# A bidirectional image scan on one core: one product for two taps of the causal convolution, and columns from blocks of 32

## The chip, the cores and the metric

The kernel runs on one core of a Trainium2 chip. The metric is the device time of one execution in microseconds. A profiled execution gives one trace; its span runs from the first instruction of the program to the last.

## The reference, cut to what matters

Layer 0 scans every image of `x` (8 images, 64 channels, 128 x 128) along its rows and along its columns, each in both directions:

```python
def mamba(seq, p):                       # seq: sequences x 128 tokens x 64
    xz = einsum('blc,ec->ble', seq, in_w)
    x, z = xz[..., :di], xz[..., di:]    # di = 128
    x = silu(causal_conv(x, conv_w, conv_b))      # 4 taps along the sequence, per channel
    xdbl = einsum('bld,ed->ble', x, xp_w)
    dt, Bm, Cm = split(xdbl)                       # 4, 16, 16 wide
    delta = softplus(einsum('blr,dr->bld', dt, dt_w) + dt_b)
    # per token: h = exp(delta*A)*h + (delta*x)*B ;  y = <h, C> + x*D    (16 states a channel)
    y = selective_scan(x, delta, -exp(A_log), Bm, Cm, Dp) * silu(z)
    return einsum('bld,cd->blc', y, out_w)
def run_bidir(seq, p):
    return 0.5 * (mamba(seq) + flip(mamba(flip(seq))))
x_rec = 0.5 * (rows(run_bidir) + columns(run_bidir))
x = silu(group_norm(x_rec)) + x
```

Layer 1 is a residual block of two 3 x 3 convolutions with batch norm on the result. All is float32. The input projection `in_w` and the four taps of `causal_conv` are both linear in the tokens, so their composition is four products, each with the tokens shifted by 0 to 3.

## The kernel before, in words

Work is cut into chunks of four sequences (`SEQ`), 512 tokens (`N`). An image has 32 row chunks and then 32 column chunks (`NCH` = 32), so there are 512 chunks in all. A chunk has 16 steps: step r takes one pair of channel halves (`half`), one group of four states (`ng`) and one direction (`d`) by `where(r)`. The loop `for s in range(total + UN)` issues the steps in an order written out by hand, and every engine runs its own instructions in that order. In text below, a step's number in brackets says for which step a piece of work is done: `drive(10)` is the drive for step 10.

For each step there are:

- `decay`: ScalarE (ACT) writes the edge (L360) and two exponentials (L363) into `dA`, one of two PSUM buffers, one step ahead of the scan. It may start once the scan two steps before has read its `dA`.
- `drive`: VectorE (DVE) multiplies `du` by `pb`, B spread over the partitions (L372), one step ahead. For steps 2, 5, 9, 12 and 15 (`GPS`) GpSimd (POOL) does it, from `bt`, which a DMA brings.
- `scan`: DVE scans 1024 elements (L380 forward, L382 backward).
- `weigh`: POOL multiplies the states by C (L387).
- `b_rows`, in even steps for the two steps that follow: TensorE makes `pb` (L352), into the one PSUM buffer of the tag "b". It waits until the last reader of that buffer is done.
- `add_up`, in even steps, four steps behind: TensorE sums states into `yp` (L403).

Beside the steps of chunk n, `prepare` makes what chunk n+1 needs, one piece per step from step 0 to 13:

- step 0: for a column chunk, ACT copies the chunk's columns out of the image in SBUF, `xc` (L252);
- steps 1 to 4: the products `cp` (L234 for rows, L240 for columns, called in `project`), two taps of one direction in each step;
- step 5: `u` (SiLU of `cp`, L265) and SiLU of the chunk's `sz`; step 6: `dp` (L272); step 7: `bp` (L277, tag "b") and its copy `bc` by ACT (L282), which a DMA stores as `bd` (L284);
- step 8: softplus (L287); step 9: `du` by DVE (L299), `dl` by ACT (L301) and eight DMAs to `dd` (L294); steps 10 to 13: eight DMAs that bring `dl` and `du` back, each channel repeated four times (L323); step 13: `zp` (L240 or L234, tag "b") and its copy `sz` (L314).

`cp`, `dp`, and the outputs `op` and `cps` share one PSUM buffer of two banks (tag "pt"). In step 3 DVE gates the chunk before (`y`, L410), in step 4 TensorE begins the next `yp` with u times D (`dg`, L393), and at steps 10 to 12 the chunk before is projected out: `op` (L416; for columns L421 adds what the rows left), copies by ACT (L429, L434), and for columns statistics by DVE (`gst`, L438). Group norm and the first convolution (`conv1`, L493 to L507) of the image before run in steps 5 and 7, and 14 to 2, of row chunks.

The whole image lies in SBUF as `xt`, the lower half of its rows on partitions 64 to 127, so a product takes 128 partitions of which the weights of one half are zero; a column chunk takes two products per tap, one for each half of the rows. The next image is loaded in the last two chunks. Nearly all DMAs are issued on SyncE's (SP's) queue, in program order; `fetch` brings `c` and `bt` some steps ahead.

## Time and profile before

| | |
|---|---|
| runs, median (lowest to highest) | 27046.4 us (27022.64 to 27052.52), 3 runs |
| profiled execution, its own time | 27036.85 us |
| its span, mean granted TensorE clock | 27035.1 us, 0.878 |
| busy: DVE, POOL, PE, ACT | 25638.5, 25139.5, 19433.8, 18477.9 us |
| products `cp`: L234 (rows), x4096 | 2022.6 us, 617 ns each |
| products `cp`: L240 (columns), x8192 | 2068.0 us, 397 ns each |
| copy `xc`, L252, x256 | 159.4 us, 623 ns each |
| DMA queues, share of 16 engines | 51.9% on SP's, 180 GB/s over the span |

A row of the profile names line, engine, operation, output and inputs, and how often. The busy time is the union of a group's instructions; the mean is of one, and instructions overlap, so count times mean can exceed it. A product in float32 appears as two records. "Idle" is the time in which the engine did nothing just before an instruction, and the name behind the arrow is what ended it. The scans run from 126 to 25907 us; what follows is the tail of the last image and layer 1's second convolution.

### The profile page before, as it was taken

To read this page: it belongs to the slowest core of one execution; us is meant where nothing else is said; L and a number is where in the kernel's file an instruction comes from. 1 tells how busy PE (TensorE), PEld (TensorE's weight loads), DVE (VectorE), ACT (ScalarE), POOL (GpSimd) and SP (SyncE) were. 2 spreads that over 40 slices of the span, in tenths; PEclk is the share of its full clock that TensorE was granted. 3 is DMA by queue.
4 is the path that set the end of the run, shared out by engine and by line. 5 is a ranking of instruction groups with operands and counts; after the bars stand their busy time and mean duration, and the time that the engine had idled before them with its cause. 6 is when DMAs were issued, how large, how long until landed. Compare 5 with 4: busy or idle time off the path is not lost.

```text
span 27035.1 us, 235698 instructions
## 1 busy us (share of the span) xinstructions
PE 19433.8 (72%) x65580; PEld 6667.4 (25%) x65580; DVE 25638.5 (95%) x15633; ACT 18477.9 (68%) x31150; POOL 25139.5 (93%) x10916
## 2 busy tenths in 40 slices
PE   5777777777777777777777777777777777777776
PEld 1222222222222222222222222222222222222222
DVE  8999999999999999999999999999999999999942
ACT  5777777777777777777777777777777777777732
POOL 7999999999999999999999999999999999999930
PEclk8888888888988889888898888988898888988888
DMA  5555555555555555555555555555555555555545
GB/s 180 174 180 172 184 191 183 177 173 184 194 179 176 172 189 192 178 174 172 194 188 177 175 177 193 184 181 171 179 197 178 178 173 182 198 177 179 170 141 188
DMA packets 2165564, 4871.20 MB, mean 180 GB/s; under 512 B 265856, under 2 KB 413456, under 8 KB 2148368
## 3 DMA queue, kind: packets, MB, share of 16 engines
q1 hardware_dynamic: 2143648, 4754.51, 51.9%
q10 hardware_dynamic: 15984, 68.06, 0.9%
q0 software_dynamic: 4608, 33.56, 0.3%
q8 instruction: 517, 8.47, 0.1%
q14 instruction: 807, 6.61, 0.1%
HBM read 4115.52 MB, written 738.98 MB: 180 GB/s over the span
## 4 chain that ended last, share of the span: by engine, by line
DVE 35%; PE 22%; issue 18%; ACT 12%; DMA 9%; SPq 2%; POOL 1%; DVEq 0%; POOLq 0%; ACTq 0%
DVE s L372 15%; DVE s L382 9%; DVE s L380 8%; DMA du<-dd 7%; PE pb L352 6%; ACT dA L363 6%; PE yp L403 5%; PE cps L665 2%; PE dp L272 2%; DVE du L299 2%; PE op L421 1%; PE op L416 1%; DVE y L410 1%; PE bp L277 1%; ACT xp L434 1%
## 5 line engine op out<-in xcount | busy, mean ns | idle before, releaser
L387 POOL TENSOR_TENSOR s<-s,c 128x1024 f32<-128x1024 f32 x8192 | 19151.8, 2365 | 659.6 <-DVE s L382 290.8
L363 ACT ACTIVATE dA<-dl,A 128x508 f32<-128x508 f32 x16384 | 11274.9, 688 | 518.0 <-ACT dA L360 3.1
L352 PE MATMUL pb<-u,wb 128*128 128x512 f32 x8192 | 5455.4, 753 | 6516.4 <-DVE s L372 5728.6
L382 DVE TENSOR_TENSOR_SCAN s<-dA,s 128x1024 f32<-128x1024 f32 x4096 | 9284.9, 2276 | 45.2 <-ACT dA L363 42.1
L380 DVE TENSOR_TENSOR_SCAN s<-dA,s 128x1024 f32<-128x1024 f32 x4096 | 9281.8, 2276 | 0.0
L372 DVE TENSOR_TENSOR s<-du,pb 128x1024 f32<-128x1024 f32 x5632 | 6742.2, 1197 | 132.7 <-DMA du<-dd 88.4
L372 POOL TENSOR_TENSOR s<-du,bt 128x1024 f32<-128x1024 f32 x2560 | 6071.0, 2371 | 149.6 <-DMA bt<-bd 147.3
L403 PE MATMUL yp<-s,fold 128*32 128x512 f32 x32768 | 5196.3, 712 | 5.2 <-POOL s L387 5.2
L360 ACT COPY dA<-zeros 128x8 f32<-128x8 f32 x8192 | 1381.9, 169 | 5321.8 <-DVE s L382 3465.4
L352 PEld LDWEIGHTS pb<-u,wb 128*128 128x128 f32 x8192 | 1522.2, 219 | 9638.4 <-DVE s L372 3874.8
L234 PE MATMUL cp<-xt,wc 128*128 128x512 f32 (+3 forms) x4096 | 2022.6, 617 | 119.1 <-DMA xt<-x_h 76.7
L240 PE MATMUL cp<-xc,wc 128*128 128x256 f32 (+3 forms) x8192 | 2068.0, 397 | 0.0
L240 PEld LDWEIGHTS cp<-xc,wc 128*128 128x128 f32 x8192 | 1585.9, 199 | 1029.5 <-issue 459.6
L403 PEld LDWEIGHTS yp<-s,fold 128*32 128x32 f32 x32768 | 692.5, 116 | 3780.4 <-issue 1996.7
L363 ACT ACT_TABLE_LOAD x1030 | 1321.5, 1283 | 26.7 <-DMA dl<-dd 8.4
L234 PEld LDWEIGHTS cp<-xt,wc 128*128 128x128 f32 x4096 | 766.7, 198 | 1424.5 <-issue 1242.4
L272 PE MATMUL dp<-u,wd 128*128 128x512 f32 x2048 | 983.5, 603 | 1.2 <-ACT u L265 1.2
L393 PE MATMUL yp<-u,dg 128*128 128x512 f32 x2048 | 961.9, 592 | 1.7 <-DVE y L410 1.7
L694 POOL DMA_DIRECT2D out<-cc x32 | 17.2, 538 | 979.0 <-ACT cc L693 979.0
L434 ACT COPY xp<-op 64x256 f32<-64x256 f32 x512 | 317.5, 620 | 887.6 <-PE op L421 884.6
L416 PE MATMUL op<-y,wo 128*128 128x512 f32 x1024 | 821.8, 895 | 0.9 <-DVE y L410 0.9
L493 PE MATMUL cps<-strip,w 128*128 128x512 f32 x1536 | 770.9, 629 | 48.9 <-DMA strip<-x_d 41.1
(109 smaller groups left out, 10548.3 us busy)
## 6 DMA issues: line engine op xcount, KB each, us to landing
dl<-dd SPq DMA_DIRECT2D x2048, 512.0 KB
du<-dd SPq DMA_DIRECT2D x2048, 512.0 KB
c<-bd SPq DMA_DIRECT2D x4096, 256.0 KB
bt<-bd SPq DMA_DIRECT2D x2560, 256.0 KB
dd<-du SPq DMA_DIRECT2D x2048, 128.0 KB
dd<-dl SPq DMA_DIRECT2D x2048, 128.0 KB
bd<-bc SPq DMA_DIRECT2D x512, 128.0 KB
c_d<-cs SPq DMA_DIRECT2D x256, 256.0 KB
```

Of the source, the lines that this page charges most:

```text
L234: nc.tensor.matmul(ps[:, :, lo:hi], lhsT[hf], xt[:, r : r + SEQ, lo - s : hi - s], start=start, stop=stop)
L240: nc.tensor.matmul(ps[:, :, lo:hi], lhsT[hf], g["xc"][:, :, lo - s - hf * HH : hi - s - hf * HH], start=start and hf == 0, stop=stop and h ...
L272: nc.tensor.matmul(dp[:, d, :], w["wd"], u[:, d, :], start=True, stop=True)
L352: nc.tensor.matmul(pb, wt[g["o"]]["wb"][:, P * ng : P * (ng + 1)], g["u"][:, d, :], start=True, stop=True)
L360: nc.scalar.copy(dA[:, :, :, edge], zeros)
L363: nc.scalar.activation(dA[:, j, :, t], dl[:, j, :, t], AF.Exp, scale=wt[g["o"]]["A"][:, 2 * half + j, ng : ng + 1])
L372: engine.tensor_mul(s, g["du", half, d], b.unsqueeze(1).to_broadcast([P, 2, N]))
L380: nc.vector.tensor_tensor_scan(s, a, s, 0.0, ALU.mult, ALU.add)
L382: nc.vector.tensor_tensor_scan(s[:, ::-1], a[:, ::-1], s[:, ::-1], 0.0, ALU.mult, ALU.add)
L387: nc.gpsimd.tensor_mul(s, s, c.unsqueeze(1).to_broadcast([P, 2, N]))
L403: nc.tensor.matmul(g["yp"][32 * q : 32 * (q + 1), :], fold, s[:, j, :], start=False, stop=r == UN - 2, skip_group_check=True,)
L416: nc.tensor.matmul(op, w["wo"].rearrange("p h c -> p (h c)"), g["y"], start=True, stop=o == 0)
```

## The change

A chunk's tokens no longer come from an image in SBUF. `stack` writes them twice into `xs`, one of two buffers that chunks use in turn: on partitions 0 to 63 as they are and on partitions 64 to 127 a token later, with columns of zeros on both sides. A product over 128 partitions then makes two taps, with weights laid out to match (`shift`), and a direction takes two products, whether rows or columns. `zp` takes the lower 64 partitions alone.

For a row chunk the two copies are DMAs from DRAM. For a column chunk ACT copies the columns to `xc` (`columns`, now at the head of step 0 of the chunk two before, ahead of `decay`), and four DMAs carry them to the stack. They are issued in step 2 of the chunk two before. The columns come from blocks of 32 (`CB`), two of which lie in SBUF; `load_columns` brings a quarter of a block at step 4 of every second chunk, from image chunk 22 on. In `prepare` the first three pieces are empty, and the products stand in steps 3 and 4. `xt` and its loads are gone.

```diff
--- before
+++ after
@@ -19,6 +19,7 @@
 HH = W // 2
 N = 512
 SEQ = N // W
+CB = 32
 NCH = W // SEQ
 NS = 16
 NQ = 4
@@ -26,7 +27,13 @@
 NTAP = 4
 EPS = 1e-5
 LAG = 4
+PAD = 2
 GPS = (2, 5, 9, 12, 15)
+
+
+def shift(d, k, e):
+
+    return 2 * k + e if d == 0 else 2 * k + 1 - e
 
 
 @with_exitstack
@@ -75,15 +82,15 @@
             cw = prep.tile([P, NTAP, P], F32, name="cw")
             nc.scalar.dma_start(out=cw, in_=p["conv_wT"].partition_broadcast(P))
 
-            wc = const.tile([P, 2, NTAP, P], F32, name=f"wc{o}")
-            wz = const.tile([P, 2, P], F32, name=f"wz{o}")
-            nc.vector.memset(wc, 0.0)
-            nc.vector.memset(wz, 0.0)
-            for hf in range(2):
-                h = slice(hf * C, (hf + 1) * C)
-                for j in range(NTAP):
-                    nc.vector.tensor_mul(wc[h, hf, j, :], inw[h, 0:P], cw[h, j, :])
-                nc.vector.tensor_copy(wz[h, hf, :], inw[h, P : 2 * P])
+
+            wc = const.tile([P, 2, 2, P], F32, name=f"wc{o}")
+            for d in range(2):
+                for k in range(2):
+                    for e in range(2):
+                        h = slice(e * C, (e + 1) * C)
+                        nc.vector.tensor_mul(wc[h, d, k, :], inw[h, 0:P], cw[h, NTAP - 1 - shift(d, k, e), :])
+            wz = const.tile([C, P], F32, name=f"wz{o}")
+            nc.vector.tensor_copy(wz, inw[0:C, P : 2 * P])
 
             xpr = prep.tile([4, P], F32, name="xpr")
             nc.sync.dma_start(out=xpr, in_=p["xp_w"][0:4, :])
@@ -210,57 +217,67 @@
         psa = st.enter_context(tc.tile_pool(name="psa", bufs=1, space=PSUM))
         psm = st.enter_context(tc.tile_pool(name="psm", bufs=1, space=PSUM))
 
-        xt = big.tile([P, HH, W], F32, name="xt")
         xp = big.tile([P, HH, W], F32, name="xp")
         strips = []
         for k in range(2):
             strip = big.tile([P, SEQ + 1, W + 2], F32, name=f"strip{k}")
             nc.vector.memset(strip, 0.0)
             strips.append(strip)
+        stacks = []
+        for k in range(2):
+            xs = big.tile([P, SEQ, PAD + W + 3], F32, name=f"xs{k}")
+            nc.vector.memset(xs, 0.0)
+            stacks.append(xs)
         zeros = big.tile([P, 2, SEQ], F32, name="zeros")
         nc.vector.memset(zeros, 0.0)
 
-        def load_image(b, k):
-
-            rows = slice(k * (HH // 8), (k + 1) * (HH // 8))
-            nc.sync.dma_start(out=xt[:, rows, :], in_=x[b].rearrange("p (h w) -> p h w", w=W)[:, rows, :])
-
-        def project(ps, lhsT, g, s, start, stop):
-
-            ps = ps.rearrange("p (q t) -> p q t", t=W)
-            if g["o"] == 0:
-                hf, r = divmod(SEQ * g["i"], HH)
-                lo, hi = max(s, 0), W + min(s, 0)
-                nc.tensor.matmul(
-                    ps[:, :, lo:hi], lhsT[hf], xt[:, r : r + SEQ, lo - s : hi - s], start=start, stop=stop
-                )
-                return
-            for hf in range(2):
-                lo, hi = max(hf * HH + s, 0), min((hf + 1) * HH + s, W)
-                nc.tensor.matmul(
-                    ps[:, :, lo:hi], lhsT[hf], g["xc"][:, :, lo - s - hf * HH : hi - s - hf * HH],
-                    start=start and hf == 0, stop=stop and hf == 1, skip_group_check=True,
-                )
+        def load_columns(b, k, j):
+
+            if j == 0:
+                blocks[b, k] = big.tile([P, HH, CB], F32, name="xb", bufs=2)
+            rows = slice(j * (HH // 4), (j + 1) * (HH // 4))
+            nc.sync.dma_start(
+                out=blocks[b, k][:, rows, :],
+                in_=x[b].rearrange("p (h w) -> p h w", w=W)[:, rows, CB * k : CB * (k + 1)],
+            )
+
+        def columns(g):
+
+            if g["o"] == 1:
+                k, i = divmod(SEQ * g["i"], CB)
+                g["xc"] = work.tile([P, SEQ, HH], F32, name="xc", bufs=1)
+                nc.scalar.copy(g["xc"], blocks[g["b"], k].rearrange("p h w -> p w h")[:, i : i + SEQ, :])
+
+        def stack(g, k):
+
+            xs = g["xs"] = stacks[k % 2]
+            for e in range(2):
+                es = slice(e * C, (e + 1) * C)
+                if g["o"] == 0:
+                    hf, r = divmod(SEQ * g["i"], HH)
+                    src = x[g["b"]].rearrange("p (h w) -> p h w", w=W)[hf * C : (hf + 1) * C, r : r + SEQ, :]
+                    nc.sync.dma_start(out=xs[es, :, PAD + e : PAD + e + W], in_=src)
+                else:
+                    for hf in range(2):
+                        t = PAD + e + hf * HH
+                        nc.sync.dma_start(out=xs[es, :, t : t + HH], in_=g["xc"][hf * C : (hf + 1) * C])
 
         def prepare(g, before):
 
 
             w = wt[g["o"]]
-            if g["o"] == 1:
-                g["xc"] = work.tile([P, SEQ, HH], F32, name="xc", bufs=1)
-                i = SEQ * g["i"]
-                nc.scalar.copy(g["xc"], xt.rearrange("p h w -> p w h")[:, i : i + SEQ, :])
+            yield
+            yield
             yield
             cp = psm.tile([P, 2, N], F32, name="cp", tag="pt")
             for d in range(2):
-                for s in range(NTAP):
-                    j = NTAP - 1 - s
-                    project(
-                        cp[:, d, :], [w["wc"][:, 0, j, :], w["wc"][:, 1, j, :]], g,
-                        s if d == 0 else -s, s == 0, s == NTAP - 1,
+                for k in range(2):
+                    t = PAD - 2 * k if d == 0 else PAD + 2 * k + 1
+                    nc.tensor.matmul(
+                        cp[:, d, :].rearrange("p (q t) -> p q t", t=W), w["wc"][:, d, k, :],
+                        g["xs"][:, :, t : t + W], start=k == 0, stop=k == 1,
                     )
-                    if s % 2:
-                        yield
+                yield
             u = work.tile([P, 2, N], F32, name="u")
             nc.scalar.activation(u, cp, AF.Silu, bias=w["conv_b"])
             if before is not None:
@@ -309,7 +326,9 @@
             replicate(g, 0, 1)
             yield
             zp = psa.tile([P, N], F32, name="zp", tag="b")
-            project(zp, [w["wz"][:, 0, :], w["wz"][:, 1, :]], g, 0, True, True)
+            nc.tensor.matmul(
+                zp.rearrange("p (q t) -> p q t", t=W), w["wz"], g["xs"][0:C, :, PAD : PAD + W], start=True, stop=True
+            )
             g["sz"] = work.tile([P, N], F32, name="sz")
             nc.scalar.copy(g["sz"], zp)
             replicate(g, 1, 1)
@@ -517,7 +536,7 @@
         OUT = 10
         NORM = (5, 7)
         CONV = (14, 15, 0, 1, 2)
-        LOAD = (2, 4, 6, 8)
+        blocks = {}
         gs = [dict(b=b, o=o, i=i) for b in range(B) for o in range(2) for i in range(NCH)]
         total = UN * len(gs)
         stats = {}
@@ -540,8 +559,8 @@
             return 2 if r == GPS[0] else 3
 
         with tc.manual_schedule():
-            for k in range(8):
-                load_image(0, k)
+            stack(gs[0], 0)
+            stack(gs[1], 1)
             for _ in prepare(gs[0], None):
                 pass
             for s in range(-9, 0):
@@ -557,6 +576,8 @@
                     for _ in pieces:
                         pass
                     pieces = prepare(gs[n + 1], gs[n]) if n + 1 < len(gs) else iter(())
+                if r == 0 and n + 2 < len(gs):
+                    columns(gs[n + 2])
                 if s + 1 < total:
                     decay(*at(s + 1))
                     if (s + 1) % UN not in GPS:
@@ -586,8 +607,10 @@
                 fetch(s)
                 if r == CONV[-1] and n % PER == 6:
                     next(conv3, None)
-                if r in LOAD and live and n % PER >= PER - 2 and gs[n]["b"] + 1 < B:
-                    load_image(gs[n]["b"] + 1, LOAD.index(r) + 4 * (n % 2))
+                if r == 2 and n + 2 < len(gs):
+                    stack(gs[n + 2], n + 2)
+                if r == 4 and n % 2 == 0 and NCH - 10 <= n % PER < PER - 10:
+                    load_columns(n // PER, *divmod((n % PER - NCH + 10) // 2, 4))
                 if r == OUT and prev:
                     output = emit(prev)
                     next(output)
```

## The prediction

> **What bounds the kernel now.** I read the page's busy shares first, then who waits for whom, then the timeline of single chunks. Over the span:

> ```profile
> PE 19433.8 (72%) x65580; PEld 6667.4 (25%) x65580; DVE 25638.5 (95%) x15633; ACT 18477.9 (68%) x31150; POOL 25139.5 (93%) x10916
> PEclk8888888888988889888898888988898888988888
> ```

> Between the first scan (126 us) and the last (25907 us) DVE is busy for 25382 us of 25781: it is the bound, POOL (25097) is just behind it, and TensorE has slack. The starts of the scans give 49.07 us as the shortest chunk. So a change to TensorE's work counts only through DVE's waits, some 400 us in all:

> ```profile
> DVE gst L438 <- ACT xp L434: 225.0, 209, 4.1
> DVE s L372 <- DMA du<-dd: 88.4, 124, 11.4
> DVE s L382 <- ACT dA L363: 42.1, 112, 0.4
> DVE s L372 <- PE pb L352: 32.6, 94, 1.5
> ```

> (total us, times, longest.) The last row is what the change aims at: mostly `drive(4)` waiting for its `pb`, which TensorE starts late behind the `cp` products of steps 1 and 2.

> ```profile
> 2232.41 1.10 PE L352 MATMUL pb<-u,wb 128*128 128x512 f32 x2 [1.81 <-DVE s L372]
> 2233.34 1.88 PE L272 MATMUL dp<-u,wd 128*128 128x512 f32 x4
> 2236.03 1.03 PE L277 MATMUL bp<-u,xpT 128*32 128x512 f32 x4
> ...
> 17266.57 1.74 PE L352 MATMUL pb<-u,wb 128*128 128x512 f32 x2 [1.86 <-DVE s L372]
> 17268.10 2.97 PE L272 MATMUL dp<-u,wd 128*128 128x512 f32 x4
> 17271.89 1.03 PE L277 MATMUL bp<-u,xpT 128*32 128x512 f32 x4
> ```

> (start, us, what; in brackets the idle time before.) With 1.81 us of idleness before step 6 the products ran at full clock; with 1.86 us they ran slow, `bp` came 1.7 us later, and ACT and DVE show who paid:

> ```profile
> 17272.96 0.58 ACT L282 COPY bc<-bp 64x512 f32<-64x512 f32 x1 [2.06 <-PE bp L277]
> 17274.83 1.22 DVE L372 TENSOR_TENSOR s<-du,pb 128x1024 f32<-128x1024 f32 x1 [0.72 <-PE pb L352]
> ```

> The windows of busy time confirm the clock (the column before the last two):

> ```profile
> 2232.40:2237.10 4.70, 4.65 (x18) 1.42 (x18) 4.70 (x3) 4.22 (x8) 4.70 (x3) 1.00 0.00 0
> 17266.90:17270.30 3.40, 3.40 (x5) 1.35 (x4) 3.40 (x3) 3.29 (x6) 3.40 (x3) 0.50 0.00 0
> ```

> The path: `bp` holds the one buffer of tag "b" until ACT has copied it to `bc` (L282); only then `pb` for `drive(10)` may be written (L352), and DVE needs it. Besides the first chunk, 18 chunks in the trace had `bp` 1.24 to 1.70 us late, and DVE waited 0.25 to 0.72 us: a late `bp` costs its lateness less 0.98 us.

> [...]the trace's packets of 512, 256 and 4 bytes took 27, 15 and 9 ns[...].

> **The change, part by part.**

> *Products.* Before, `cp` is 16 records per chunk of 0.43 us (row, L234), or 32 of half the width (column, L240), 6.9 us at full clock, in four pieces at steps 1 to 4. After, it is 8 records, 3.4 us, in two pieces at steps 3 and 4. Direct gain: the waits for `pb` at step 2, by the trace 26.6 us of the 32.6. Indirect cost: the freed time becomes idleness just before step 6. Count t from the scan of step 0. At 5.6 TensorE gets to `pb(4)`; behind it stand `yp`, `cp`, `pb(6)`, `cp`, `dg`, `yp`: 1.0+1.0+1.8+1.0+1.8+1.8+1.0 = 9.4 us at full clock, so it ends at 15.0 and not at 16.6 as now. `pb(8)` can't start before `drive(7)` ends at 18.4. The idleness grows from 1.81 to 3.4 us, over the 1.9 that one window bears; `dp`, `yp` and `bp` then start at half clock.

> How often: at step 0 TensorE mostly comes out of a pause at half clock (0.53 in column chunks, 0.72 in row chunks). Its `pb` and `yp` then fill t = 0.2 to 4.3. A window fills to 0.86 if it begins between -0.24 and 1.36, 1.6 of 3.41 us: in 47% of chunks the clock is full by `pb(4)`. In the other 53% it rises only at t = 8.7 to 12, the half-speed time fills the pause, and step 6 runs at full clock as now; `pb(4)` at half clock takes 2.07 us, inside the scan's 2.28, so it costs nothing. In the 47%, the fifth window edge lies at 16.8 to 18.4, where the clock drops (not in some 5% of them). Edges after 17.95 (30%) leave a full window next: one slow window, `bp` 1.5 to 1.7 late, 0.6 us of stall as in the 18 chunks. The other 65% wait two windows, 5.2 to 6.3 us at half speed: 2.6 to 3.15 late, 1.9 us of stall. Mean: 0.47 x (0.30 x 0.6 + 0.65 x 1.9) = 0.67 us per chunk; for the 376 chunks without conv1's products 250 us. In the 128 chunks with them (image chunks 7 to 22) TensorE is more often at full clock by step 2 but also busier until then; bounds 0 and 0.95 us, I take 0.3: 38 us.

> *Copy xc* (L252, 623 ns x256) goes ahead of step 1's decay on ACT. ACT then idles 1.14 us until DVE's scan frees `dA`, so zero; uncovered, 160 us. Its one buffer was read 14 steps earlier.

> *DMAs.* Gone: 64 loads of `xt`, 512 KB. New, all on SP's queue: two of 128 KB per row chunk, four of 64 KB per column chunk, 128 block loads of 256 KB in 128-byte runs. SP spends some 0.5 us on an issue, 1 to 2.5 us per chunk; it waits 7389.5 us (511 times, 14.5 each) at L284 for `bc`, and the new issues stand before that point. Behind them stand `c` for steps 8 to 12, `bt` and `bd`; `c` waits for a buffer from POOL anyway. A column stack makes SP wait for ACT's copy of step 0, before the time at which `c(8)` gets its buffer; that the stack's own buffer be free takes `zp` of chunk n, done at step 13 of the chunk before. Each DMA also waits for the one eight places ahead of it in SP's order (eight semaphores in turn); between `bd` and `du<-dd` nothing is put in, so the critical stretch keeps its neighbours. Ring time over 16 engines: 512 x 27 ns = 0.9 us (row), 1024 x 15 = 1.0 us (column)[...]. They run around steps 1 to 4, eight steps before `dd` and the critical `du` (88.4 us of waits). Zero; bounds 0 and 500 us below.

> *Start and preparation.* The first `cp` waits for `xt` until 91.7 us and takes 10.07 us for 16 records; with 8 it ends about 5 us sooner, less 1 us for clearing the stacks (two memsets like `strip`'s 0.6 us): -4 us, bounds -6 and 0. DVE's fewer clears of weights lie beside the load of `p_w`: zero. The freed SBUF: zero.

> Sum: 250 + 38 - 27 - 4 = +257 us. The profiled execution took 27036.85 us, 9.6 below the median; 27294 by its own time, 27300 as a median.

> **The rivals.**
> *No change (17%).* TensorE isn't done early enough: it needs under 1.86 us of idleness before step 6. That is so if it enters step 2 at half clock in nearly every phase. Then -31 us, 27015. Against it: a clock of 0.97 to 0.99 in step 2.
> *Faster (13%).* The wait of `gst` (0 to 1.33 us) also hangs on where windows fall: five column chunks take 252.6 us, just 74 windows, so chunks lock to the grid. If the new pattern locks where the mean wait is 0.5 and not 0.88, 100 us go, and 31 as above: 26915. It decides where chunks of 49.55 us keep clear of the slow phases, and needs step 6's delay to be absent.
> *Slower by DMA (7%).* The new transfers push `du` by about 1 us in every chunk: 512 us, 27550. It decides only if they are still in the rings at step 10.
> If the stacks don't halve the products, PE's instructions would not fall; the instruction lists show `cp` at two per direction.

> **Numbers.** The likeliest case is 63%, 27300, its own range 27100 to 27480. With the rivals, 26990 to 27480. A measurement here tells about 0.2% (54 us) from no change: faster 0.16, same 0.18, slower 0.66.

> **What would show it.** The products' 4090.6 us (L234 and L240) fall to 512 x 3.44 = 1760, more where the clock is half, and PE's busy time to some 17100 to 17900; the waits for `pb` at step 2 vanish; ACT's wait for `bp` (176.8 us) rises over 500, DVE's wait for `pb` (32.6) to about 300, now at `drive(10)`; TensorE idles over 3 us before step 6 in half of the chunks, and the mean clock (0.878) falls. I'm wrong on the cause if `bp` is hardly ever late, or if DVE's longer wait is the one for `du`; wrong on the size if late `bp` is seen in far more or fewer than 47% of chunks, or mostly with one slow window.

## The result, and the profile after

The changed kernel takes 27359.22 us (median of 4 runs, 27340.04 to 27373.71), against 27042.92 us before (4 runs, 27022.64 to 27052.52). The ratio is 1.0118, with a 95% interval of 1.0105 to 1.0131: slower by 316 us, where 254 were forecast. The profiled execution has a span of 27371.9 us, 336.8 more than the one before.

The page of the changed kernel begins with the busy times, and shows the clock in forty slices:

```profile
PE 18899.4 (69%) x56876; PEld 5233.6 (19%) x56876; DVE 25699.2 (94%) x15629; ACT 18459.6 (67%) x31150; POOL 25149.2 (92%) x10916
PEclk8888888888888888888888888888888888888888
```

TensorE has 8704 records fewer but is busy for only 534 us less, since much of what is left runs slower: `pb`, `yp` and `dp` together are busy for 1224 us longer (L371, L422 and L289, before L352, L403 and L272). The mean clock fell from 0.878 to 0.830. DVE, the bound, is busy for 61 us more with no more work.

Who waits for whom on DVE, the rows that answer to those of before (total us, times, longest):

```profile
DVE s L391 <- PE pb L371: 279.3, 221, 2.1
DVE gst L457 <- ACT xp L453: 240.3, 254, 4.1
DVE s L391 <- DMA du<-dd: 79.1, 95, 11.6
DVE s L401 <- ACT dA L382: 36.2, 112, 0.4
```

One wait has grown much, that of `drive` for `pb`, from 32.6 to 279.3 us; the wait of `gst` for `xp` is 15 us longer, that of `drive` for `du` 9 us shorter. On ACT, the row for the copy that stands between `bp` and `pb` rose from 176.8 us to:

```profile
ACT bc L299 <- PE bp L294: 717.3, 478, 3.4
```

The timeline of TensorE in one row chunk, from `pb(4)` to `bp`, shows how that comes about. Steps 2 to 4 are one unbroken block at full clock (1.00 from 8118.52 to 8127.87 us); then comes a pause, in brackets, and then `pb(8)` and `dp` at half clock:

```profile
8118.52 1.12 PE L371 MATMUL pb<-u,wb 128*128 128x512 f32 x2 [1.49 <-DVE s L391]
8119.58 1.06 PE L422 MATMUL yp<-s,fold 128*32 128x512 f32 x8
8120.57 1.99 PE L276 MATMUL cp<-xs,wc 128*128 128x512 f32 x4
8122.41 1.02 PE L371 MATMUL pb<-u,wb 128*128 128x512 f32 x2
8123.26 1.89 PE L276 MATMUL cp<-xs,wc 128*128 128x512 f32 x4
8124.99 1.88 PE L412 MATMUL yp<-u,dg 128*128 128x512 f32 x4
8126.80 1.07 PE L422 MATMUL yp<-s,fold 128*32 128x512 f32 x8
8131.33 2.04 PE L371 MATMUL pb<-u,wb 128*128 128x512 f32 x2 [3.47 <-DVE s L391]
8133.17 3.62 PE L289 MATMUL dp<-u,wd 128*128 128x512 f32 x4
8136.72 1.40 PE L422 MATMUL yp<-s,fold 128*32 128x512 f32 x8
8137.95 1.02 PE L294 MATMUL bp<-u,xpT 128*32 128x512 f32 x4
```

`pb(8)` takes 2.04 us and `dp` 3.62 us, about twice as long as in the usual chunk of before (1.10 and 1.88). The windows of busy time give the clock, in the column before the last two, for the stretch from `pb(8)` to the start of `bp` and for the one after:

```profile
8131.40:8138.00 6.60, 6.60 (x16) 2.10 (x18) 6.57 (x4) 4.14 (x7) 6.60 (x4) 0.54 0.00 0
8138.20:8140.50 2.30, 1.62 (x6) 0.30 (x2) 0.81 (x1) 1.41 (x4) 2.30 (x2) 1.00 0.00 0
```

What ACT and DVE wait for in the same chunk:

```profile
8139.02 0.58 ACT L299 COPY bc<-bp 64x512 f32<-64x512 f32 x1 [3.36 <-PE bp L294]
8140.89 1.22 DVE L391 TENSOR_TENSOR s<-du,pb 128x1024 f32<-128x1024 f32 x1 [1.88 <-PE pb L371]
```

The stretch from the first scan to the last is 333 us longer (25780 to 26113), and two sums make this up. DVE's idle time there grew by 271 us (399 to 670). Its idle time in front of `drive(10)`, counted by step, rose from 8 to 292 us; that in front of `drive(4)`, which the prediction calls the wait at step 2, was 27 us and is gone. DVE's busy time there grew by 62 us (25381 to 25443); the last section says why.

### The profile page after: what moved, and what is told of

Its sections match the earlier page's. It is cut to its first block, busy times and chain, and to the rows that moved or that the text cites. A ratio compares the mean times of both kernels' runs of the same rounds, so it can differ in the third digit from the quotient of the medians.

```text
span 27371.9 us, 221652 instructions
## 1 busy us (share of the span) xinstructions
PE 18899.4 (69%) x56876; PEld 5233.6 (19%) x56876; DVE 25699.2 (94%) x15629; ACT 18459.6 (67%) x31150; POOL 25149.2 (92%) x10916
## 5 line engine op out<-in xcount | busy, mean ns | idle before, releaser
L382 ACT ACTIVATE dA<-dl,A 128x508 f32<-128x508 f32 x16384 | 11274.5, 688 | 518.6 <-DMA dl<-dd 2.0
L371 PE MATMUL pb<-u,wb 128*128 128x512 f32 x8192 | 5988.2, 821 | 7418.6 <-DVE s L391 6648.1
L391 DVE TENSOR_TENSOR s<-du,pb 128x1024 f32<-128x1024 f32 x5632 | 6748.9, 1198 | 384.9 <-PE pb L371 279.3
L422 PE MATMUL yp<-s,fold 128*32 128x512 f32 x32768 | 5519.5, 753 | 5.2 <-POOL s L406 5.2
L371 PEld LDWEIGHTS pb<-u,wb 128*128 128x128 f32 x8192 | 1581.2, 233 | 11407.7 <-DVE s L391 5262.2
L276 PE MATMUL cp<-xs,wc 128*128 128x512 f32 x4096 | 2097.8, 634 | 79.5 <-DMA xs<-x_h 79.5
L422 PEld LDWEIGHTS yp<-s,fold 128*32 128x32 f32 x32768 | 715.4, 120 | 4249.8 <-issue 2461.0
L289 PE MATMUL dp<-u,wd 128*128 128x512 f32 x2048 | 1351.5, 797 | 1.2 <-ACT u L282 1.2
L276 PEld LDWEIGHTS cp<-xs,wc 128*128 128x128 f32 x4096 | 784.7, 203 | 1515.7 <-issue 1423.9
L329 PE MATMUL zp<-xs,wz 64*128 64x512 f32 x1024 | 581.8, 647 | 583.5 <-DVE s L391 582.8
L453 ACT COPY xp<-op 64x256 f32<-64x256 f32 x512 | 317.4, 620 | 915.9 <-PE op L440 912.9
L299 ACT COPY bc<-bp 64x512 f32<-64x512 f32 x512 | 296.4, 579 | 717.3 <-PE bp L294 717.3
```

The source lines that it names most:

```text
L276: nc.tensor.matmul(cp[:, d, :].rearrange("p (q t) -> p q t", t=W), w["wc"][:, d, k, :], g["xs"][:, :, t : t + W], start=k == 0, stop=k == 1,)
L289: nc.tensor.matmul(dp[:, d, :], w["wd"], u[:, d, :], start=True, stop=True)
L371: nc.tensor.matmul(pb, wt[g["o"]]["wb"][:, P * ng : P * (ng + 1)], g["u"][:, d, :], start=True, stop=True)
L382: nc.scalar.activation(dA[:, j, :, t], dl[:, j, :, t], AF.Exp, scale=wt[g["o"]]["A"][:, 2 * half + j, ng : ng + 1])
L391: engine.tensor_mul(s, g["du", half, d], b.unsqueeze(1).to_broadcast([P, 2, N]))
L422: nc.tensor.matmul(g["yp"][32 * q : 32 * (q + 1), :], fold, s[:, j, :], start=False, stop=r == UN - 2, skip_group_check=True,)
```

## The experiments

The theory is that of the prediction: a longer pause of TensorE before step 6, half clock, a late `bp`, and a wait of DVE at `drive(10)`. The rival is that the new DMAs, the earlier copy or SP's longer queue cost the time. A further question is whether holding the clock also shortens the wait of `gst`, which both kernels have.

The table gives each kernel's ratio to the kernel before on the same chip. The products issued twice, the one and the two zero products and the fills in 5, 8 and 9 ran on a chip where the kernel before took 27040.53 us; the DMAs issued twice, half of the taps and the fills in 8 and 9 on one where it took 27028.62 us. So kernels are compared by their ratios. From the trace the table gives how often the pause before step 6 was over 1.88 us and how often `bp` was over 0.5 us later than in a usual chunk of before, both of 511 chunks, and DVE's idle time before `drive(10)`.

| kernel | median us | ratio, 95% interval | long pauses | late `bp` | idle at `drive(10)`, us |
|---|---|---|---|---|---|
| before | 27042.92 | 1 | 9 | 19 | 8 |
| after | 27359.22 | 1.0118 (1.0105 to 1.0131) | 279 | 253 | 292 |
| after, products twice | 27020.36 | 0.9993 (0.9984 to 1.0001) | 4 | 2 | 1 |
| after, one zero product | 27079.85 | 1.0013 (1.0006 to 1.0020) | 267 | 111 | 50 |
| after, two zero products | 27014.74 | 0.9991 (0.9983 to 1.0000) | 0 | 20 | 0 |
| the same, new DMAs twice | 27000.59 | 0.9990 (0.9984 to 0.9997) | 0 | 20 | 0 |
| before, half of the taps | 27354.89 | 1.0120 (1.0105 to 1.0135) | 285 | 252 | 290 |
| after, fills in 5, 8 and 9 | 26818.15 | 0.9918 (0.9903 to 0.9932) | 0 | 32 | 0 |
| before, fills in 8 and 9 | 26811.57 | 0.9920 (0.9903 to 0.9936) | 8 | 15 | 7 |

The clock records tie the last three columns together. In the changed kernel the clock was at half somewhere between the start of `pb(8)` and the end of `bp` in 253 chunks, and these are the 253 with a late `bp`. The late ones of the three kernels with two zero products in step 5 (20, 20 and 32) have another cause, which the records here don't show: their clock was full in this stretch in every chunk, and DVE didn't wait.

### The changed kernel, its products issued twice

```diff
-            yield
-            yield
             yield
             cp = psm.tile([P, 2, N], F32, name="cp", tag="pt")
             for d in range(2):
-                for k in range(2):
...
+                for again in range(2):
+                    for k in range(2):
...
+                    yield
-                yield
```

> The changed kernel, with the products of steps 3 and 4 issued twice (steps 1 and 2 for the first direction, 3 and 4 for the second), so that TensorE has as many cp records as the kernel before and everything else is as after the change; the result is the same values written again. Theory (the halved products leave TensorE idle before step 6 and its clock halves): the idleness before step 6 is back under 1.9 us, DVE's wait for pb at step 8 falls from 279 us to under 40, the waits for pb at step 2 come back, and the time is about 27040 us (26990 to 27090). Rival (the new DMAs, the copy or SP's longer queue cost the time): 27360 us, since none of them is touched.

Measured: 27020.36 us, ratio 0.9993. DVE's wait for `pb` is 26.9 us in all, and its idle time in front of `drive(4)` is 23 us. All the loss is gone although nothing but TensorE's work, and the steps in which it stands, was changed; the DMAs, the copy and the longer queue stayed. The time is within the range given, 20 us under its middle. (The records of `cp` are 8192 of 512 columns; the kernel before has 4096 of about this width and 8192 of half of it, so the work is the same and the count isn't.)

### One, and two, products of zero weights in step 5

The edit with two products (with one, the count is 1):

```diff
+        zw = big.tile([P, P], F32, name="zw")
+        nc.vector.memset(zw, 0.0)
...
+                if live:
+                    for _ in range({5: 2}.get(r, 0)):
+                        nc.tensor.matmul(
+                            gs[n]["yp"], zw, gs[n]["u"][:, 0, :], start=False, stop=False, skip_group_check=True
+                        )
                 if r in NORM and n % PER:
```

> The changed kernel with one product of zero weights (128x512, two records, 0.86 us at full clock) added into yp in step 5, which changes no value. Theory: the idleness before step 6 shrinks from 3.4 to about 2.55 us, still over the 1.9 us that a window bears in most positions of the grid; the clock drops in about two thirds of the cases it does now: 27150 to 27300 us. Rival (DMAs or SP): 27360 us.

> As the one before, with two such products in step 5 (1.7 us). Theory: idleness before step 6 about 1.7 us, under the threshold, as in the kernel before; the late bp goes, and what is left is the change's own gain: about 27010 us (26960 to 27060), DVE's wait for pb under 30 us. If [...]DMAs or SP were the cause: 27360 us.

Measured with two: 27014.74 us, 5 us from what was expected. This row is what is left of the wait for `pb`:

```profile
DVE s L393 <- PE pb L373: 5.5, 14, 0.6
```

Measured with one: 27079.85 us, better than the 27150 to 27300 that were expected. The pauses over 1.88 us are nearly as many as without a fill (267 against 279), but `bp` was late in only 111 chunks, 44% of the 253 and not two thirds, and only in 6 by more than 2.2 us, against 144 without. The clock records show why so few waited for two slow windows: without a fill, half of the late cases had the drop 1.01 us or more before `pb(8)` began; with one product, in half of them it came 0.18 us or more after. So the cost fell faster with the length of the pause than I took it to, and 0.86 us of filling removes 280 of 316 us. Of the 111, 84 lie in the 119 chunks that also hold products of `conv1`.

### The changed kernel with two zero products, the new DMAs issued twice

```diff
-            nc.sync.dma_start(
...
+            for _ in range(2):
+                nc.sync.dma_start(
+                    out=blocks[b, k][:, rows, :],
...
-                    stack(gs[n + 2], n + 2)
+                    for _ in range(2):
+                        stack(gs[n + 2], n + 2)
```

> The changed kernel with two zero products in step 5, and each of the new DMAs (stacks and blocks) issued twice. Theory (the transfers lie in time that SP and the rings have free): no different from the run with the two products alone, 27015 us (26980 to 27060), DVE's wait for du near 94 us. Rival (the new transfers cost something that the fill only hid): as much again as they cost now, 27050 us and more.

Measured: 27000.59 us, ratio 0.9990 beside 0.9991 with the DMAs once. DVE's wait for `du`:

```profile
DVE s L394 <- DMA du<-dd: 86.5, 113, 10.9
```

It was 93.6 us (125 times) without the doubling. The new transfers cost nothing that can be seen where they stand, and neither do twice as many. ACT's copy was not doubled; that it costs nothing either rests on the kernels with the products twice and with two zero products, which keep it and are no slower than the kernel before.

### The kernel before, half of its taps left out

```diff
+            yield
+            yield
             cp = psm.tile([P, 2, N], F32, name="cp", tag="pt")
             for d in range(2):
-                for s in range(NTAP):
+                for s in range(2):
                     j = NTAP - 1 - s
                     project(
                         cp[:, d, :], [w["wc"][:, 0, j, :], w["wc"][:, 1, j, :]], g,
-                        s if d == 0 else -s, s == 0, s == NTAP - 1,
+                        s if d == 0 else -s, s == 0, s == 1,
                     )
-                    if s % 2:
-                        yield
+                yield
```

> The kernel before, image in SBUF and its DMAs untouched, with two of the four taps left out of each direction and the remaining products in steps 3 and 4: as much TensorE time for cp as after the change, and none of the change's DMAs. It leaves out half of the convolution's taps, so its output is another one. Theory (less TensorE work alone lets the clock fall before step 6): as slow as the changed kernel, 27360 us (27290 to 27430), with DVE's wait for pb near 280 us. Rival (the halved products need the new transfers or the stack's waits to do harm): 27010 us.

Measured: 27354.89 us, ratio 1.0120, the changed kernel's 1.0118 within the intervals, and the same wait:

```profile
DVE s L373 <- PE pb L353: 274.0, 232, 1.9
```

This kernel has the image in SBUF, the old DMAs and the old copy; it only does less on TensorE, and is slower by as much. So less work on TensorE is enough, without the rest of the change. It also gathers its products in steps 3 and 4, as the changed kernel does, so it doesn't tell the amount of the work from its place. What both come to is the pause, and the zero products change the pause alone.

### Fills before step 10 as well, in both kernels

```diff
-                    for _ in range({5: 2}.get(r, 0)):
+                    for _ in range({5: 2, 8: 2, 9: 3}.get(r, 0)):
```

In the kernel before, the same with `{8: 2, 9: 3}` and with `ident` as weights and `zeros[:, 0, 0:1].to_broadcast([P, N])` as data.

> As the one before, and five more zero products (two in step 8, three in step 9, 4.3 us) in the 5.7 us of idleness before step 10. Theory: op then runs at full clock, so the wait of gst for xp at step 12 (240 us after the change) falls under 30 us, of which the wait for du at the next step 0 takes back up to 70 us: about 26830 us (26760 to 26920). Rival (gst waits for something other than the clock): no better than the run with two products alone.

> The kernel before, with five products of zeros (two in step 8, three in step 9) added into yp, changing no value. Theory: the wait of gst (225 us) goes as it did in the changed kernel, some of it comes back as a wait for du: about 26870 us (26800 to 26930). What is left between this and the changed kernel with both fills (26818 us) is what the change is worth once the clock is held: 30 to 50 us. Rival (the fills helped only because of the stacks): no gain over 27043 us.

Measured: 26818.15 us for the changed kernel and 26811.57 us for the one before. The group of `gst` on DVE, in the kernel before, and in the changed kernel with the fills (busy time, mean ns, then idle time before it):

```profile
L438 DVE BATCH_NORM_STATS2 gst<-xp 128x6 f32<-128x256 f32 x256 | 109.4, 427 | 225.7 <-ACT xp L434 225.0
```

```profile
L459 DVE BATCH_NORM_STATS2 gst<-xp 128x6 f32<-128x256 f32 x256 | 102.2, 399 | 4.1 <-ACT xp L455 4.1
```

The wait of `gst` is gone, in the kernel before with its fills too (4.1 us). What `gst` waits for is ACT's copy of `op`, and the products `op` are where the clock shows (shortest, median and longest in ns, the changed kernel without and with the fills):

```profile
L435 PE MATMUL op<-y,wo x1024: 592/869/1222, 212.2 to 26246.9; 128*128 128x512 f32 x171
L437 PE MATMUL op<-y,wo x1024: 592/697/1222, 211.5 to 25698.9; 128*128 128x512 f32 x171
```

In the changed kernel without fills, those of these records that began and ended at full clock took 592 to 697 ns, and those at half clock 1222 in the median; 31% began at full clock, and 38% in the one before. With the fills ACT's wait for `op` in column chunks fell from 912.9 to 300.3 us in the changed kernel and from 884.6 to 299.7 in the one before.

In the changed kernel, of the 230 us that `gst` waited with two zero products alone, the wait for `du` took back 18 (93.6 to 111.8) and the wait for `pb` 31 (5.5 to 36.7, nearly all at the `drive(0)` that follows). The kernel before came out 58 us under what I expected. Some 14 us of this are the chip, on which it takes 27028.62 us and not 27043; besides, its wait for `du` stayed at 87.4 us, where I had let it grow. Both kernels are faster than the kernel before without fills, by 0.8%. I had given the change 30 to 50 us between the two. The ratios differ by 0.0002, about 5 us; but each interval is some 0.15%, 40 us, to either side, so a gain of this size is neither shown nor excluded.

## Why the prediction was right, point by point

- *DVE is the bound, and TensorE counts only through DVE's waits*: so it was. TensorE lost a fifth of its loading of weights (6667.4 to 5233.6 us) and 534 us of busy time, and the kernel got slower.
- *The mechanism* was the one named: pause, half clock, late `bp`, late `pb`, wait at `drive(10)`. The kernel with half of the taps shows it without the rest of the change, and the two zero products, which only fill the pause, take it away.
- *The clock's records*: in the traces of the kernel before and of the changed one, every stretch at 1.0 or 0.5, but for the one that the end cuts off, lasts a whole number of 3413 ns. The trace of the kernel before has 1092 drops and 1093 rises between the first scan and the last, where the prediction counts 987. Over all of them its bounds hold: a window before a drop was at most 0.50 busy, one before a rise at least 0.83, and one that kept the clock full over 0.42. The last section has windows of other kernels that fall outside them.
- *The pause* was forecast at 3.4 us. It was 3.47 us in the chunk shown, and over 3 us in 247 of 511 chunks.
- *Chunks with conv1's products*: the prediction counted 128 of them, and 376 without. The trace has 119, image chunks 6 to 22 of seven images, since there is no image before the first; 392 are without. I took 0.3 us each, with bounds of 0 and 0.95; they cost 0.64, in all 76 us in place of 38.
- *How often*: forecast 47% of chunks, less some 5% of these; `bp` was late in 253 of 511, 49.5%. This agreement is in part luck. The 47% was worked out for chunks without conv1's products, and there it was 154 of 392, 39%; with them it was 99 of 119. The working took the edges of the clock's windows as spread evenly, but the chunks lock to them: in 286 of the 392 an edge falls in the same 1.02 us of the 3.41, counted from the scan of step 0. The clock was full by `pb(4)` in 234 of the 392, more than 47%, and only 132 of these had a late `bp`.
- *One or two slow windows*: outside conv1's chunks, one was forecast in 30 of 95 cases, with 0.6 us of stall, and two in 65, with 1.9. There 37 of the 154 were late by up to 2.2 us and 117 by more, with stalls of 0.53 and 1.67 us on average. So two windows were a little more frequent and every stall a little cheaper: 216 us, where the sum had 250.
- *The size*, then, is right because errors cancel: 292 us of idle time at `drive(10)`, 288 forecast.
- *Gain at step 2*: 27 us were forecast, and 27 are gone. *Start*: 4 us were forecast; the first scan comes 0.8 us earlier, which is no more than kernels with the same start differ by (123.3 to 125.1 us in the five that begin like the changed one). The first `cp` takes 6.2 us in place of 10.1, but begins 2.3 us later, behind the loading of the stacks.
- *Copy and DMAs at zero*: right, for the DMAs by doubling them, for the copy as said there. SP still waits long for `bc` (7658.3 us, 7389.5 before), so the new issues find room in front of it.
- *What the sum lacked*: 62 us of DVE's busy time. The idle time that it forecast, 261 us without the start, was 271; with the 62 this makes the 333 us of the stretch. That 257 lies 59 us under the 316 between the medians comes mostly from this term.
- *TensorE's busy time* was put at 17100 to 17900 us and is 18899: I counted half clock for `cp` alone, not for the `pb`, `yp` and `dp` that follow the pause.
- *The rivals*: the block that isn't done early enough ("no change") and a better lock to the windows ("faster") did not come about; the wait of `gst` is much as before. "Slower by DMA" fell with the doubled DMAs.

## What to carry to other kernels

Before taking work off an engine that isn't the bound, ask what its idle time will do. Here TensorE's products were what kept its clock up for the next, urgent ones (full from `pb(8)` to `bp` in all 511 chunks with two zero products, in 258 without), and 3.4 us less of them per chunk cost 0.6 us of the bound. The mean clock doesn't tell this: the version with two zero products has a mean of 0.849, less than the 0.878 before, and is no slower. What counted is the clock in the stretch in front of the wait that DVE feels. Two products that add zero, put before step 6, repaired the change, and five more before step 10 took both kernels to 0.8% under the kernel before.

## What the runs showed of the hardware that I had not expected

- A wait on DVE cost more than its idle time. Instructions in a row overlapped (in the chunk shown a scan of 2.28 us is followed after 2.20), and one that waited didn't overlap the one before. The single instructions of the scan stretch add up to 26550 us before and 26552 after; their overlaps add up to 1169 us and to 1108. That is the 62 us. Over the nine kernels DVE's busy time in this stretch follows 25305 us plus 0.108 us for each idle gap, within 10 us, with 499 to 1285 gaps. The changed kernel has 524 gaps more, of which 381 are under 0.1 us themselves; most stand at `drive(8)`, `drive(10)` and the scan of step 11.
- Products whose weights, or whose data, are all zero kept the clock up: with two of zero weights in the pause the clock was full from `pb(8)` to `bp` in all 511 chunks, against 258 without, and before `op` either kind worked, zero weights in the changed kernel and zero data in the one before (`gst` waits 4.1 us in both).
- A product over 64 partitions was no shorter than one over 128. At full clock the two records of `zp` together took 1124 ns over 64 (505 products of the changed kernel) and 1125 over 128 (248 of the row chunks before); the loads of its weights took 186 and 189 ns.
- But it counted for less with the clock. In the three kernels whose `zp` reads 128 partitions, no window after which the clock dropped was over 0.505 busy, as in the prediction. In the six whose `zp` reads 64, there are 671 drops after windows that were over 0.505 and up to 0.63 busy, and each of these windows holds `zp`. If `zp` is counted at half there, no drop of the six lies above 0.50, and no window that kept the clock full lies under 0.41 (0.493 and 0.416 in the changed kernel). It stands in step 13, and DVE's waits don't show it: in the kernel with the products twice, which has it too, `gst` waits 223.9 us, beside 225.0 before.
- The changed kernel's 262144 packets of 128 bytes took 13 ns in the median; by that, an estimate, the 2048 of a block load come to 1.7 us over the 16 engines. Those of 256 bytes took 21 in the changed kernel, which has 264448 of them, and 15 before, where there were 2304.
